# A capacity mixture that sends its results to the tokens' rows, and an attention whose loads and norms are reordered

## The chip, the cores and the metric

One core of a Trainium2 chip runs the whole program in one launch. The metric is the device time in microseconds: the median of three runs. Five engines matter below: TensorE (PE), VectorE (DVE), ScalarE (ACT), GpSimd (POOL) and SyncE (SP), which issues most DMAs.

## The reference

Four layers over x (4 x 256 tokens of 256 numbers), each of an attention and a feed-forward part on a layer norm, both added to x. The context has 4 x 1601 tokens. The parts that matter here:

```python
# layer 2, feed-forward: T = 1024 tokens, E = 8 experts, C = T / E = 128 seats each, H = 352
probs = softmax(xt @ Wg); eidx = argmax(probs); gate = probs[eidx]
oh = one_hot(eidx); pos = (cumsum(oh, 0) * oh).sum(-1) - 1      # first come, first served
keep = pos < C
flat = where(keep, eidx * C + pos, E * C)
xd = zeros(E * C, d).at[flat].set(xt, mode='drop').reshape(E, C, d)
oe = ((silu(xd @ W1) * (xd @ W3)) @ W2).reshape(E * C, d)       # an expert at a time
out = take(oe, minimum(flat, E * C - 1)) * (gate * keep)[:, None]
return out + (silu(xt @ sw1) * (xt @ sw3)) @ sw2                # a shared expert beside it

# layer 3, attention: 16 query heads, 4 key heads, head size 128
q = rms_norm(x @ Wq); k = rms_norm(ctx @ Wk); v = ctx @ Wv      # 4 query heads share a key head
y = softmax(q @ k.T / sqrt(128)) @ v @ Wo
```

Layer 1's attention is of the same kind, with the tokens of x behind the context's as keys, and with queries and keys turned by their position (rope). Layer 0 has an attention that keeps 54 scores a row and a top-2 mixture, layer 1 a linear map, layer 2 an attention of 16 heads of 16 to an image part and a text part of the context, and layer 3 a top-2 mixture with a shared expert.

## The kernel before

x stays on the chip as eight tiles `X[j]` of 128 tokens. The stages follow one another: the first attention with its mixture to about 520 us of the profile, `gqa` for layer 1 ("l1a", 520 to 1870), the linear map, the image and text attention (to 2467), `capacity_moe` (2467 to 2569), `gqa` for layer 3 ("l3a", 2570 to 3690) and the last mixture. In the stages touched here the order on PE, ACT and DVE is that of the program (`manual_schedule`; in `gqa` POOL's as well). SP's queue, and POOL's in `capacity_moe`, are ordered by a scheduler. An engine and a queue take their work strictly in order.

**The layer norm.** `normed(nat)` gives the transposed tiles `xT` and, for each of four pairs of token tiles, three steps: statistics with the reciprocal root (DVE, one pow on POOL by `rsqrt`, L122, DVE scales into `nat`, L145), PE's transposes, and the copies out of PSUM. `layernorm()` runs all of them at once.

**`capacity_moe`.** It loads the router's `wg`, the shared expert's weights `wsh` and eight experts' weights (1088 KB each), norms the four pairs into `nat[0..7]`, routes, and counts each token's seat with two PE products. `ix` gets two rows for each token tile: the seat's row, or a row past the seats for a token that found none, and the same clamped to 1023. Eight indirect stores, issued by POOL (L1897), send the tiles' rows to XD in DRAM, and eight plain loads bring an expert's 128 rows back (`xs`, L1905). Meanwhile PE runs the shared expert's first products (`up`, L1866) and first half of its second (`down(0)`). Then, one expert ahead of the other, `hidden(e)` (transposes, L1916, products L1924, silu) and `project(e)` (L1937); ACT copies the result (`oe`, L1939) and SP stores it to OE in DRAM (L1940). `down(1)` adds the shared expert's second half to `X[4..7]`. Then eight indirect loads from POOL's queue (L1951) fetch each token's row from OE, and DVE adds it, times `gate`, to `X[j]` (L1954). `gate` has been set to zero for tokens without a seat.

**Between the stages.** The last mixture's shared weights `shw` (1536 KB) are loaded first, then `layernorm()` runs, some constants are made on POOL, and `gqa` starts. `send_to_shared` gives `gqa` the hook `others`, through which the last mixture's routing is hung into its slots.

**`gqa`.** Its 16 units are a batch times a key head. A unit has four steps: a tile of 128 tokens by a pair of query heads. A step takes four slots, and a slot runs its phases in the order first, early, mid, late, last, values, pe, post: "mid" holds the row maxima (DVE, L1252) and the exponentials (ACT, L1253) of this slot's scores (PE, L1244, into three score banks `sc0..2`); `combine` (L1290 to L1298) joins the parts of the softmax and turns the blocks; `values` (L1324) multiplies by the values; the last product with `wo` is L1337. `at(slot, phase, f)` hangs anything into a slot. Slot -16 is the first, and scores start at slot -4. `produce_queries` projects (L1187), norms (`rsq`, L122; `nq`, L1208) and transposes (L1219) the queries, `produce_keys` (L1113) the keys and values. For l3a some key chunks were made in the first attention (`early`, 13, 12, 0 and 0 for the four batches) and are loaded by `load_keys`; for batch 0 these are all. `evac` copies out of PSUM, by ACT and DVE in turn. The weights of a unit:

```python
def weights(u):                                  # L1051
    for t, n in ((wkv, "_wkv"), (wq, "_wq")):
        nc.sync.dma_start(t, A[key + n]...)      # L1058: 256 KB and 512 KB for l3a's and l1a's
    nc.sync.dma_start(wo, A[key + "_wo"]...)     # 512 KB
...
weights(0); weights(1)                           # ahead of all slots; later units in a slot
```

Of the kernel before, what the change touches and what calls it, by code (L numbers as in the profile page):

```python
# [12 lines left out]
F32 = mybir.dt.float32  # L13
I32 = mybir.dt.int32
# [4 lines left out]
P = 128  # L19
B = 4  # L20
# [32 lines left out]
def kernel(ctx: ExitStack, tc: tile.TileContext, A, out: bass.AP):  # L53
# [70 lines left out]
    def normed(nat=None, bank=None):  # L124


        halves = []

        def pair(i):
            v = {}  # L130

            def scale():
                if i % 2 == 0:
                    halves.append(pools["x"].tile([P, NC_, 512], F32, tag="xlnT", name="xlnT", bufs=2))
                mv = small([P, 2, 2], "bnmv2")
                for tt in range(2):
                    st = small([P, 6], "bnst")
                    nc.vector.bn_stats(st, X[2 * i + tt])
                    nc.vector.bn_aggr(mv[:, tt], st)
                rstd = small([P, 2], "rstd2")  # L140
                rsqrt(rstd, mv[:, :, 1], 1.0, 1e-5, P, 2)
                v["xl"] = []
                for tt in range(2):
                    xl = nat[2 * i + tt] if nat is not None else small([P, D], "xl", 2)
                    nc.vector.tensor_scalar(  # L145
                        xl, X[2 * i + tt], mv[:, tt, 0:1], rstd[:, tt : tt + 1], ALU.subtract, ALU.mult
                    )
# [860 lines left out]
    def gqa(xT, key, tabs=None, early=None, others=None):  # L1008
# [14 lines left out]
        with (  # L1023
# [24 lines left out]
            def at(slot, phase, *fs):  # L1048
                todo.setdefault((slot, phase), []).extend(fs)

            def weights(u):  # L1051
                kv = u % KVH
                w = pool.tile([P, 1536], F32, tag="w", name="w")
                wo = pool.tile([P, GRP, D], F32, tag="wo", name="wo", bufs=3)
                wq = w[:, 0:1024].rearrange("p (c o) -> p c o", c=NC_)
                wkv = w[:, 1024:1536].rearrange("p (c o) -> p c o", c=NC_)
                for t, n in ((wkv, "_wkv"), (wq, "_wq")):
                    nc.sync.dma_start(t, A[key + n].rearrange("p (c h o) -> p c h o", c=NC_, h=KVH)[:, :, kv, :])  # L1058
                nc.sync.dma_start(wo, A[key + "_wo"].rearrange("p (k h o) -> p k h o", k=KVH, h=GRP)[:, kv])
                state[u] = dict(wq=wq, wkv=wkv, wo=wo)  # L1060

            def loaded(u):

# [285 lines left out]
            if others:  # L1349

                others(at, lambda b: 4 * (16 * b + 15) + 13)
            weights(0)
            weights(1)
            for u in range(units):
                made = -(-loaded(u) // 2)
                n = len(pairs) - made + 2
                t0 = 16 * (u - 1) - 4 if u else -13
                if made:
                    load_keys(u, t0)
                if u > 1:  # L1360
                    at(t0 - 3, "early", lambda u=u: weights(u))
                for g in range(n):
                    t = t0 + (g // 2 if u == 0 else g * 12 // n)
                    if g < 2:
                        produce_queries(u, g, t)
                    else:
                        produce_keys(u, made + g - 2, t)
# [430 lines left out]
        nc.vector.tensor_tensor(dst, psu, gv, ALU.mult)  # L1798


    def capacity_moe(XD, OE):

# [4 lines left out]
        with (  # L1807
# [3 lines left out]
        ):  # L1811
            wg = one.tile([P, NC_, E], F32, tag="wg", name="wg")
            nc.sync.dma_start(wg, A["l2f_wg"])

            def weights(tag, src):
                w = one.tile([P, 2176], F32, tag=tag, name=tag)
# [14 lines left out]
            nc.gpsimd.iota(base, [[CAP, E]], base=-1, channel_multiplier=0, allow_small_or_imprecise_dtypes=True)  # L1831
            lost = one.tile([P, NJ], F32, tag="lost", name="lost")
            nc.gpsimd.iota(lost, [[P, NJ]], base=LOST, channel_multiplier=1, allow_small_or_imprecise_dtypes=True)
            nat = [one.tile([P, D], F32, tag=f"nat{j}", name=f"nat{j}") for j in range(NJ)]
            xT, norm = normed(nat)
            norm[0][0]()
            for i in range(NJ // 2):
                if i + 1 < NJ // 2:
# [49 lines left out]
            ix = one.tile([P, 2, NJ], I32, tag="ix", name="ix")  # L1888
# [3 lines left out]
            nc.vector.tensor_tensor(ix[:, 0, :], f, lost, ALU.add)  # L1892
# [41 lines left out]
            def project(e, hT):  # L1934
                ps = ps_tr()
                for hc, (o, n) in enumerate(H2C):
                    nc.tensor.matmul(ps[:, :D], hT[:n, hc, :], W[e][2][:n, hc, :], start=(hc == 0), stop=(hc == 2))  # L1937
                oe = pool.tile([P, D], F32, tag="oe", name="oe")
                nc.scalar.copy(oe, ps[:, :D])  # L1939
                nc.sync.dma_start(OE[e * CAP : (e + 1) * CAP, :], oe)  # L1940

            hT = None
            for e in range(E + 1):
# [3 lines left out]
                hT = nx  # L1947
            down(1)
            for j in range(NJ):
                y = one.tile([P, D], F32, tag=f"xs{j}", name=f"y{j}")  # L1950
                nc.gpsimd.indirect_dma_start(  # L1951
                    y, None, OE[:, :], bass.IndirectOffsetOnAxis(ap=ix[:, 1, j : j + 1], axis=0)
                )
                nc.vector.scalar_tensor_tensor(X[j], y, gate[:, j : j + 1], X[j], ALU.mult, ALU.add)  # L1954

# [338 lines left out]
    OE = dp.tile([E * CAP, D], F32, tag="oe", name="oe")  # L2294
# [11 lines left out]
    with rings(0, sc=3, tr=1, acc=1):  # L2306
        image_text(layernorm())
    with rings(0, tr=3, acc=5):
        capacity_moe(XD, OE)
    with tc.tile_pool(name="sort3", bufs=1) as sortp:  # L2310
        shw = sortp.tile([P, 3072], F32, tag="shw", name="shw")
        nc.sync.dma_start(shw, A["l3f_sw"])
# [91 lines left out]
```

## Time and profile before

| | |
|---|---|
| median of 3 runs | 3754.8 us (3753.04 to 3756.34) |
| profiled execution | 3761.75 us, its span 3760.0 us |
| mean granted PE clock | 0.97 |
| PE / PE weight loads busy | 3557.2 us (95%) / 2128.8 us (57%) |
| DVE / ACT / POOL busy | 2615.3 (70%) / 1678.3 (45%) / 1311.5 us (35%) |
| DMA | 248.5 MB, mean 66 GB/s |
| the chain that ended last, by engine | PE 70%, DVE 14%, POOL 7%, issue 5%, ACT 2%, DMA 2% |

The profile is of one execution. Busy shares are means over stages with different limits. The chain is followed back from the last instruction: at each step to what released it, or to the instruction before it on its engine; "issue" is time in which nothing shown was waited for. The clock is the share of full speed that PE was granted.

### The profile page before, as it was taken

To read this page: it belongs to the slowest core of one execution; us is meant where nothing else is said; L and a number is where in the kernel's file an instruction comes from. 1 tells how busy PE (TensorE), PEld (TensorE's weight loads), DVE (VectorE), ACT (ScalarE), POOL (GpSimd) and SP (SyncE) were. 2 spreads that over 40 slices of the span, in tenths; PEclk is the share of its full clock that TensorE was granted. 3 is DMA by queue.
4 is the path that set the end of the run, shared out by engine and by line. 5 is a ranking of instruction groups with operands and counts; after the bars stand their busy time and mean duration, and the time that the engine had idled before them with its cause. 6 is when DMAs were issued, how large, how long until landed. Compare 5 with 4: busy or idle time off the path is not lost.

```text
span 3760.0 us, 63083 instructions
## 1 busy us (share of the span) xinstructions
PE 3557.2 (95%) x23397; PEld 2128.8 (57%) x23397; DVE 2615.3 (70%) x5204; ACT 1678.3 (45%) x4926; POOL 1311.5 (35%) x2091
## 2 busy tenths in 40 slices
PE   8887968999999999999999999987999999999998
PEld 4556954555555555555545555553555556556655
DVE  7894856777777777777667676525778766666664
ACT  4442645445444444444224444522444445545532
POOL 3332444444544544444321101012333433333332
PEclk9997989999999999999989999988999999999999
DMA  7326342222221222220100000033111111111103
GB/s 245 102 69 235 85 142 69 63 67 63 73 70 56 59 68 64 65 73 17 40 36 19 1 19 1 1 136 133 42 57 43 57 35 43 56 35 38 28 27 111
DMA packets 173715, 248.50 MB, mean 66 GB/s; under 512 B 21581, under 2 KB 134881, under 8 KB 169825
## 3 DMA queue, kind: packets, MB, share of 16 engines
q1 hardware_dynamic: 167025, 233.00, 19.9%
q0 software_dynamic: 6384, 11.47, 1.4%
q8 instruction: 186, 3.05, 0.3%
q14 instruction: 120, 0.98, 0.1%
HBM read 199.39 MB, written 45.03 MB: 65 GB/s over the span
## 4 chain that ended last, share of the span: by engine, by line
PE 70%; DVE 14%; POOL 7%; issue 5%; ACT 2%; DMA 2%; SPq 0%; another core or an unknown queue 0%; POOLq 0%; DVEq 0%; ACTq 0%
PE acc L1324 17%; PE sc L1244 15%; PE tr L1113 5%; PE sc L1657 4%; PE acc L1676 3%; PE tr L1187 3%; PE sc L1605 3%; DVE PT L1298 3%; POOL pe L1293 3%; PE acc L884 3%; POOL t L1160 2%; PE tr L1553 2%; PE tr L1337 2%; DVE m L521 2%; DVE work L523 1%
## 5 line engine op out<-in xcount | busy, mean ns | idle before, releaser
L1253 ACT ACTIVATE pe<-sc,ms 128x480 f32<-128x480 f32 (+1 forms) x1024 | 643.5, 631 | 892.7 <-DVE ms L1252 862.6
L1324 PE MATMUL acc<-PT,V 128*128 128x256 f32 (+1 forms) x3584 | 895.9, 390 | 6.9 <-ACT OT L1331 6.9
L1244 PE MATMUL sc<-KT,QT 128*32 128x480 f32 (+5 forms) x8192 | 883.1, 535 | 15.4 <-ACT pe L1253 12.1
L1293 POOL TENSOR_SCALAR pe<-pe,fac 128x480 f32<-128x480 f32 (+1 forms) x1024 | 654.8, 659 | 586.2 <-ACT pe L1253 213.7
L1324 PEld LDWEIGHTS acc<-PT,V 128*128 128x128 f32 (+1 forms) x3584 | 641.8, 190 | 349.4 <-issue 206.5
L1252 DVE TENSOR_REDUCE ms<-sc 128x1 f32<-128x480 f32 (+1 forms) x1024 | 607.9, 615 | 139.9 <-PE sc L1244 119.9
L1298 DVE STREAM_TRANSPOSE PT<-pe 128x1920 f32<-128x1920 f32 (+1 forms) x256 | 519.5, 2030 | 0.0
L1244 PEld LDWEIGHTS sc<-KT,QT 128*32 128x32 f32 x8192 | 220.9, 109 | 402.1 <-issue 321.8
L122 POOL TENSOR_TENSOR rs<-rsq_t,mhalf 128x2 f32<-128x2 f32 (+2 forms) x248 | 160.2, 646 | 568.6 <-DVE rsq_t L121 563.9
L1663 ACT ACTIVATE pt<-sc 128x1024 f32<-128x1024 f32 (+1 forms) x224 | 215.5, 962 | 280.7 <-PE sc L1657 245.9
L1113 PE MATMUL tr<-w,cx 128*128 128x256 f32 (+1 forms) x1264 | 303.5, 382 | 1.3 <-ACT nk L1129 1.3
L1619 DVE TENSOR_REDUCE mx<-sc 128x2 f32<-128x982 f32 (+2 forms) x224 | 211.6, 957 | 98.9 <-PE sc L1605 65.8
L1113 PEld LDWEIGHTS tr<-w,cx 128*128 128x128 f32 (+1 forms) x1264 | 226.7, 187 | 31.6 <-ACT nk L1129 2.0
L1657 PE MATMUL sc<-QT,KT 32*128 32x256 f32 (+1 forms) x1664 | 240.4, 403 | 0.0
L1605 PE MATMUL sc<-KT,QT 32*128 32x491 f32 (+4 forms) x1024 | 236.9, 564 | 0.0
L1253 ACT ACTIVATION_READ_ACCUMULATOR pe<-sc,ms 128x1 f32 x1024 | 199.4, 195 | 0.0
L1657 PEld LDWEIGHTS sc<-QT,KT 32*128 32x128 f32 (+1 forms) x1664 | 139.2, 182 | 92.8 <-issue 72.9
L1121 ACT ACTIVATE sq<-tr 128x128 f32<-128x128 f32 (+1 forms) x348 | 96.8, 278 | 171.5 <-PE tr L1113 166.4
L122 POOL TENSOR_TENSOR rsq<-rsq_t,mhalf 128x4 f32<-128x4 f32 x64 | 65.2, 1018 | 308.5 <-DVE rsq_t L121 308.5
L1676 PE MATMUL acc<-pt,vbuf 128*32 128x256 f32 (+1 forms) x1792 | 142.5, 391 | 0.0
L1161 DVE TENSOR_TENSOR nk<-nk,tab 128x256 f32<-128x256 f32 (+1 forms) x128 | 65.6, 513 | 100.2 <-POOL t L1160 99.0
L1187 PE MATMUL tr<-w,xlnT 128*128 128x512 f32 x256 | 126.1, 618 | 3.8 <-DMA wo<-in_l1a_wo 3.1
(430 smaller groups left out, 4774.5 us busy)
## 6 DMA issues: line engine op xcount, KB each, us to landing
cx<-in_ctxT SPq DMA_DIRECT2D x144, 256.0 KB, 3.0
tab<-rope SPq DMA_DIRECT2D x112, 256.0 KB, 2.7
w<-in_l0f_w SPq DMA_DIRECT2D x8, 2048.0 KB, 19.8
ctxT<-in_ctxT SPq DMA_DIRECT2D x7, 1601.0 KB, 6.5
w<-in_l2f_w SPq DMA_DIRECT2D x8, 1088.0 KB, 8.2
w<-in_l1a_wq SPq DMA_DIRECT2D x16, 512.0 KB
wo<-in_l1a_wo SPq DMA_DIRECT2D x16, 512.0 KB, 4.8
w<-in_l3a_wq SPq DMA_DIRECT2D x16, 512.0 KB, 7.3
```

The lines of the kernel that those rows point to most:

```text
L122: nc.gpsimd.tensor_tensor(dst, t[:n, :k], mhalf[:n, :k], ALU.pow)
L1113: nc.tensor.matmul(v["ps"][:n, i, :], lhs, st["wkv"][:, c, :], start=(c == 0), stop=(c == NC_ - 1))
L1187: nc.tensor.matmul(v["ps"], xtok(xT, b * 2 + tt, c), state[u]["wq"][:, c, :], start=(c == 0), stop=(c == NC_ - 1))
L1244: nc.tensor.matmul(sc[32 * r : 32 * r + 32, 0 : lens[r]], st["QT"][:, tt, o : o + 32], st["KT"][:, r, 0 : lens[r]], start=True, stop=True,)
L1252: nc.vector.tensor_reduce(top, sc, AX.X, ALU.max, negate=True)
L1253: nc.scalar.activation(w, sc, AF.Exp, bias=top, accum_out=s)
L1293: nc.gpsimd.tensor_scalar(w, w, v["fac"][:, g * 4 + a : g * 4 + a + 1], 1.0, ALU.mult, ALU.mult)
L1298: nc.vector.transpose(state[steps[i]][:, :, g * P : (g + 1) * P].rearrange("p k (a t) -> p a k t", a=4), pes[g].rearrange("p a (k i) -> p ...
L1324: nc.tensor.matmul(v["ps"][:, 0 : 2 * P], V[:n, k, :], PT[:n, k, :], start=(k == 0), stop=(k == nch - 1))
L1605: nc.tensor.matmul(st[:, j, c : c + n], QT[r, g, tt * P : (tt + 1) * P], KT[r, g, o : o + n], start=True, stop=True,)
L1657: nc.tensor.matmul(st[:n, j, q, :], KT[r, g, o : o + n], QT[r, :], start=True, stop=True)
L1676: nc.tensor.matmul(acc[32 * j : 32 * j + 32, a, :], V[:n, place, h * VW : h * VW + 32], pt[:n, j, q, :], start=(k == 0), stop=(k == nch - ...
```

## The change

In `capacity_moe` a seat's row in DRAM is longer by four numbers and carries the token's index and its gate beside its norm. The rows go to XS, whose rows were of that length already. An empty seat reads, from a store that precedes, an index past the tokens and a gate of zero. The expert's result is scaled by the gate as ACT copies it, and an indirect store from POOL, one an expert, sends its rows to the tokens' rows of XD, which a store of zeros has cleared. At the end eight plain loads, on SP's and ACT's queues in turn, fetch the token tiles' rows, and DVE adds them to `X[j]`. OE is gone, and so is the second row of `ix`.

In `gqa`, for both attentions that use it, a unit's loads go out as `wq`, `wkv`, `wo`; `wkv` only where the unit makes keys of its own. Units 0 and 1: `wq` and `wkv` of unit 0 at once, its `wo` and all of unit 1 at slot -12.

Between the two, only the first pair of tiles is normed ahead of l3a. The other three stand in its slots: statistics in "late" of slots -3, 1 and 5, the transposes in "pe" of the slot behind, the copies in "early" of the one after that. `shw` is loaded at slot 12.

```diff
@@ gqa, weights
-                for t, n in ((wkv, "_wkv"), (wq, "_wq")):
-                    nc.sync.dma_start(t, ...)
-                nc.sync.dma_start(wo, ...)
+                for t, n in ((wq, "_wq"), (wkv, "_wkv")):
+                    if n == "_wq" or 2 * -(-loaded(u) // 2) < nch:
+                        nc.sync.dma_start(t, ...)
+                return lambda: nc.sync.dma_start(wo, ...)
@@ gqa
-            weights(0)
-            weights(1)
+            at(-12, "early", weights(0), lambda: weights(1)())
...
-                    at(t0 - 3, "early", lambda u=u: weights(u))
+                    at(t0 - 3, "early", lambda u=u: weights(u)())
@@ capacity_moe
+            none = one.tile([P, E, 2], F32, tag="none", name="none")
+            nc.gpsimd.memset(none, 0.0)
+            nc.gpsimd.iota(none[:, :, 0], [[CAP, E]], base=B * S, channel_multiplier=1, ...)
+            nc.sync.dma_start(XS[0:LOST, D : D + 2].rearrange("(e p) d -> p e d", p=P), none)
+            zero = one.tile([P, D], F32, tag="zero", name="zero")
+            nc.gpsimd.memset(zero, 0.0)
+            nc.sync.dma_start(XD[0 : B * S, :]..., zero.unsqueeze(1).to_broadcast([P, NJ, D]))
...
-            nat = [one.tile([P, D], F32, tag=f"nat{j}", name=f"nat{j}") for j in range(NJ)]
-            xT, norm = normed(nat)
+            nat = [one.tile([P, ROW], F32, tag=f"nat{j}", name=f"nat{j}") for j in range(NJ)]
+            for j in range(NJ):
+                nc.gpsimd.iota(nat[j][:, D : D + 1], [[0, 1]], base=j * P, channel_multiplier=1, ...)
+                nc.gpsimd.memset(nat[j][:, D + 2 :], 0.0)
+            xT, norm = normed([t[:, 0:D] for t in nat])
...
+            for j in range(NJ):
+                nc.gpsimd.tensor_copy(nat[j][:, D + 1 : D + 2], gate[:, j : j + 1])
...
-            nc.vector.scalar_tensor_tensor(f, row, 1.0 - LOST, line, ALU.add, ALU.mult)
-            nc.vector.tensor_scalar(ix[:, 1, :], f, LOST - 1.0, 1.0, ALU.add, ALU.mult)
-            nc.vector.tensor_tensor(gate, gate, line, ALU.mult)
             for j in range(NJ):
                 ins = nc.gpsimd.indirect_dma_start(
-                    XD[:, :], bass.IndirectOffsetOnAxis(ap=ix[:, 0, j : j + 1], axis=0), nat[j], None
+                    XS[:, :], bass.IndirectOffsetOnAxis(ap=ix[:, j : j + 1], axis=0), nat[j], None
...
-                x = one.tile([P, D], F32, tag=f"xs{e}", name=f"xs{e}")
-                nc.sync.dma_start(x, XD[e * CAP : (e + 1) * CAP, :])
+                x = one.tile([P, ROW], F32, tag=f"xs{e}", name=f"xs{e}")
+                nc.sync.dma_start(x, XS[e * CAP : (e + 1) * CAP, :])
...
-                oe = pool.tile([P, D], F32, tag="oe", name="oe")
-                nc.scalar.copy(oe, ps[:, :D])
-                nc.sync.dma_start(OE[e * CAP : (e + 1) * CAP, :], oe)
+                oe = pool.tile([P, D], F32, tag="oe", name="oe", bufs=4)
+                nc.scalar.activation(oe, ps[:, :D], AF.Copy, scale=xs[e][:, D + 1 : D + 2])
+                to = small([P, 1], "y_to", 4).bitcast(I32)
+                nc.vector.tensor_copy(to, xs[e][:, D : D + 1])
+                nc.gpsimd.indirect_dma_start(XD[:, :], bass.IndirectOffsetOnAxis(ap=to, axis=0), oe, None)
...
             for j in range(NJ):
-                y = one.tile([P, D], F32, tag=f"xs{j}", name=f"y{j}")
-                nc.gpsimd.indirect_dma_start(y, None, OE[:, :], bass.IndirectOffsetOnAxis(ap=ix[:, 1, j : j + 1], axis=0))
-                nc.vector.scalar_tensor_tensor(X[j], y, gate[:, j : j + 1], X[j], ALU.mult, ALU.add)
+                y = one.tile([P, ROW], F32, tag=f"xs{j}", name=f"y{j}")[:, 0:D]
+                (nc.sync, nc.scalar)[j % 2].dma_start(y, XD[j * P : (j + 1) * P, :])
+                nc.vector.tensor_tensor(X[j], y, X[j], ALU.add)
@@ between the stages
-        nc.sync.dma_start(shw, A["l3f_sw"])
...
-            xT = layernorm()
+            xT, pairs = normed()
+            for f in pairs[0]:
+                f()
             k = sort_constants(sortp)
-            r, batch, others = send_to_shared(sortp, k, XS)
+            r, batch, routes = send_to_shared(sortp, k, XS)
+            def others(at, done):
+                routes(at, done)
+                at(12, "early", lambda: nc.sync.dma_start(shw, A["l3f_sw"]))
+                for p, t in zip(pairs[1:], (-3, 1, 5)):
+                    for f, slot, phase in zip(p, (t, t + 1, t + 2), ("late", "pe", "early")):
+                        at(slot, phase, f)
```

More of the change, by code (lines that the diff above doesn't have):

```diff
@@ L1056, in weights @@
                 wkv = w[:, 1024:1536].rearrange("p (c o) -> p c o", c=NC_)
-                for t, n in ((wkv, "_wkv"), (wq, "_wq")):
-                    nc.sync.dma_start(t, A[key + n].rearrange("p (c h o) -> p c h o", c=NC_, h=KVH)[:, :, kv, :])
-                nc.sync.dma_start(wo, A[key + "_wo"].rearrange("p (k h o) -> p k h o", k=KVH, h=GRP)[:, kv])
+                for t, n in ((wq, "_wq"), (wkv, "_wkv")):
+                    if n == "_wq" or 2 * -(-loaded(u) // 2) < nch:
+                        nc.sync.dma_start(t, A[key + n].rearrange("p (c h o) -> p c h o", c=NC_, h=KVH)[:, :, kv, :])
                 state[u] = dict(wq=wq, wkv=wkv, wo=wo)
+                return lambda: nc.sync.dma_start(
+                    wo, A[key + "_wo"].rearrange("p (k h o) -> p k h o", k=KVH, h=GRP)[:, kv]
+                )
             def loaded(u):
@@ L1798, in gated, with capacity_moe @@
         nc.vector.tensor_tensor(dst, psu, gv, ALU.mult)
-    def capacity_moe(XD, OE):
+    def capacity_moe(XS, XD):
         ET = mybir.EngineType
@@ L1813, in capacity_moe @@
             nc.sync.dma_start(wg, A["l2f_wg"])
+            none = one.tile([P, E, 2], F32, tag="none", name="none")
+            nc.gpsimd.memset(none, 0.0)
+            nc.gpsimd.iota(
+                none[:, :, 0], [[CAP, E]], base=B * S, channel_multiplier=1, allow_small_or_imprecise_dtypes=True
+            )
+            nc.sync.dma_start(XS[0:LOST, D : D + 2].rearrange("(e p) d -> p e d", p=P), none)
+            zero = one.tile([P, D], F32, tag="zero", name="zero")
+            nc.gpsimd.memset(zero, 0.0)
+            nc.sync.dma_start(
+                XD[0 : B * S, :].rearrange("(j p) d -> p j d", p=P), zero.unsqueeze(1).to_broadcast([P, NJ, D])
+            )
             def weights(tag, src):
@@ L1833, in capacity_moe @@
             nc.gpsimd.iota(lost, [[P, NJ]], base=LOST, channel_multiplier=1, allow_small_or_imprecise_dtypes=True)
-            nat = [one.tile([P, D], F32, tag=f"nat{j}", name=f"nat{j}") for j in range(NJ)]
-            xT, norm = normed(nat)
+            nat = [one.tile([P, ROW], F32, tag=f"nat{j}", name=f"nat{j}") for j in range(NJ)]
+            for j in range(NJ):
+                nc.gpsimd.iota(
+                    nat[j][:, D : D + 1], [[0, 1]], base=j * P, channel_multiplier=1,
+                    allow_small_or_imprecise_dtypes=True,
+                )
+                nc.gpsimd.memset(nat[j][:, D + 2 :], 0.0)
+            xT, norm = normed([t[:, 0:D] for t in nat])
             norm[0][0]()
@@ L1887, in capacity_moe @@
             nc.vector.tensor_scalar(line, line, CAP + 0.5, 1.0, ALU.is_lt, ALU.mult)
-            ix = one.tile([P, 2, NJ], I32, tag="ix", name="ix")
+            ix = one.tile([P, NJ], I32, tag="ix", name="ix")
             f = small([P, NJ], "c_f", 1)
@@ L1891, in capacity_moe @@
             nc.vector.tensor_tensor(f, f, line, ALU.mult)
-            nc.vector.tensor_tensor(ix[:, 0, :], f, lost, ALU.add)
-            nc.vector.scalar_tensor_tensor(f, row, 1.0 - LOST, line, ALU.add, ALU.mult)
-            nc.vector.tensor_scalar(ix[:, 1, :], f, LOST - 1.0, 1.0, ALU.add, ALU.mult)
-            nc.vector.tensor_tensor(gate, gate, line, ALU.mult)
+            nc.vector.tensor_tensor(ix, f, lost, ALU.add)
             for j in range(NJ):
                 ins = nc.gpsimd.indirect_dma_start(
-                    XD[:, :], bass.IndirectOffsetOnAxis(ap=ix[:, 0, j : j + 1], axis=0), nat[j], None
+                    XS[:, :], bass.IndirectOffsetOnAxis(ap=ix[:, j : j + 1], axis=0), nat[j], None
                 ).ins
@@ L1937, in project @@
                     nc.tensor.matmul(ps[:, :D], hT[:n, hc, :], W[e][2][:n, hc, :], start=(hc == 0), stop=(hc == 2))
-                oe = pool.tile([P, D], F32, tag="oe", name="oe")
-                nc.scalar.copy(oe, ps[:, :D])
-                nc.sync.dma_start(OE[e * CAP : (e + 1) * CAP, :], oe)
+                oe = pool.tile([P, D], F32, tag="oe", name="oe", bufs=4)
+                nc.scalar.activation(oe, ps[:, :D], AF.Copy, scale=xs[e][:, D + 1 : D + 2])
+                to = small([P, 1], "y_to", 4).bitcast(I32)
+                nc.vector.tensor_copy(to, xs[e][:, D : D + 1])
+                ins = nc.gpsimd.indirect_dma_start(
+                    XD[:, :], bass.IndirectOffsetOnAxis(ap=to, axis=0), oe, None
+                ).ins
+                tc.declare_no_dep(ins, group="results", reason="no two seats have the same token's row")
+                tc.add_to_no_dep_group("results", ins)
             hT = None
@@ L1949, in capacity_moe @@
             for j in range(NJ):
-                y = one.tile([P, D], F32, tag=f"xs{j}", name=f"y{j}")
[L1951 to L1954, printed above, removed]
+                y = one.tile([P, ROW], F32, tag=f"xs{j}", name=f"y{j}")[:, 0:D]
+                (nc.sync, nc.scalar)[j % 2].dma_start(y, XD[j * P : (j + 1) * P, :])
+                nc.vector.tensor_tensor(X[j], y, X[j], ALU.add)
     WIDE3 = 4 * I3 + D
@@ L2293 @@
     XD = dp.tile([2 * ROOM, D], F32, tag="xd", name="xd")
-    OE = dp.tile([E * CAP, D], F32, tag="oe", name="oe")
     OQ = dp.tile([(E + MORE) * P, D], F32, tag="oq", name="oq")
@@ L2308 @@
     with rings(0, tr=3, acc=5):
-        capacity_moe(XD, OE)
+        capacity_moe(XS, XD)
     with tc.tile_pool(name="sort3", bufs=1) as sortp:
         shw = sortp.tile([P, 3072], F32, tag="shw", name="shw")
-        nc.sync.dma_start(shw, A["l3f_sw"])
         with rings(0, sc0=1, sc1=1, sc2=1, tr=4, acc=1):
-            xT = layernorm()
+            xT, pairs = normed()
+            for f in pairs[0]:
+                f()
             k = sort_constants(sortp)
-            r, batch, others = send_to_shared(sortp, k, XS)
+            r, batch, routes = send_to_shared(sortp, k, XS)
[5 more added lines that the diff above has]
+                        at(slot, phase, f)
             gqa(xT, "l3a", early=(EARLY, KD, VD), others=others)
```

## The prediction

> **What bounds the kernel now.** I read the page first, then the chain of waits around the places the diff touches, then the queue and engine timelines there. PE is busy 95% of the span, so an edit pays only where PE stands. The seam between the capacity mixture and the next attention is such a place; its chain:
>
> ```profile
> 2554.08 2.61 PE tr L1866 x12
> ...
> 2561.03 0.95 POOL y L1951
> ...
> 2566.03 3.14 DMA y<-oe,ix
> 2569.17 0.03 issue
> 2569.19 0.49 DVE x L1954
> ...
> 2571.29 8.39 DMA w<-in_l3a_wq
> 2579.69 0.14 issue
> 2579.82 6.12 PE tr L1187 x8
> ```
>
> (start, length, what). PE's last shared product ends at 2559.28. Then eight gathers go out one by one from POOL, the last token tile is added at 2569.67, and only then do the loads of the next attention start; PE's first query projection waits for its weights until 2579.82. The SP queue shows why that load takes 8.39 us:
>
> ```profile
> 2569.81 0.33 SPq L2312 DMA_DIRECT2D shw<-in_l3f_sw  x1
> 2570.19 0.43 SPq L1963 DMA_DIRECT2D wg<-in_l3f_wg  x1
> 2570.67 0.58 SPq L1058 DMA_DIRECT2D w<-in_l3a_wkv  x1
> 2571.29 0.71 SPq L1058 DMA_DIRECT2D w<-in_l3a_wq  x1
> ```
>
> 1536 KB of `shw`, not used for 1000 us, and 256 KB of `wkv` lie ahead of it. The first attention starts alike: its `wkv` is issued at 521.70, its `wq` at 522.35, and PE's first L1187 is at 528.55, though its last norm transpose ended at 525.41.
>
> **The change, part by part.** The profiled execution took 3761.75 us (span 3760.0), 7 us over the median of the runs, 3754.8. I work out a difference against the former and take it off the latter.
>
> *Gathers out, scatters in.* The expert loop gets per expert one ACTIVATE with a scale in place of a COPY (0.37), a one-column DVE copy and an indirect store on POOL. PE carries that loop (L1924 2.92, L1937 1.30 of each 4.96 us); DVE waits 0.8 us an expert for PE, POOL has no work from 2507 to 2557. Cost nothing; uncovered, 8 x 0.3. No table load comes with it: in the first attention a Copy with a scale (`nk`, L1129) stands among exponentials without one. The last result leaves ACT at 2554.53, so its store starts at 2554.7. From start to the release of readers I take 2.4 us: the last seat store (L1897) started at 2506.01 and the loads behind it at 2508.39. The eight plain loads, four on SP and four on ACT, go out 0.43 us apart from 2557.1 and land after 1.9 (`xs<-xd`) to 2.5 us (`x<-xd`): the first at 2559.0 to 2559.6, the last at 2560.3 to 2560.9. DVE adds the shared product until 2559.74, then does eight adds of 0.42 to 0.48 (L181, L1954): the last ends at 2563.2, where it was 2569.67. Gain 6.4.
>
> *Loads in order of use.* Now only `wg` stands ahead of `wq`. 256 KB land in 3.0 to 3.1 us, 512 KB of `wo` in 4.8; I take 4.3 for `wq` alone. Issued at 2563.8 it is there at 2568.1. What comes last then is the norm: 4.83 us lay between the last add and the first pair's `xlnT` (2574.50). That chain stays (13 POOL constants, pow, scale, transposes, copy) and gets one DVE step ahead of the pow, 0.2. So `xlnT` at 2568.2, PE at 2568.4 to 2568.8: I take 11.2 of gain up to there, both parts together. `shw` goes to slot 12, where DMA is 8% busy (2626 to 2660); `wkv` is dropped for batch 0, whose keys are ready.
>
> *Norms in slots.* Pairs 1 to 3 ran under the wait for `wq`; now each stands in DVE's order at slots -3, 1 and 5 of the attention. One pair is the stretch from 2471.39 to 2474.30:
>
> ```profile
> 2471.39 0.42 DVE L138 BATCH_NORM_STATS2 bnst<-x 128x6 f32<-128x256 f32 x1
> ...
> 2472.59 0.17 DVE L121 TENSOR_SCALAR rsq_t<-bnmv 128x2 f32<-128x2 f32 x1
> 2473.56 0.74 DVE L145 TENSOR_SCALAR nat<-x,bnmv,rstd 128x256 f32<-128x256 f32 x2 [0.81 <-POOL rstd L122]
> ```
>
> 2.9 us in which DVE does nothing else, 0.8 of it waiting for POOL's pow. Queued behind are the row maxima (L1252), behind them ACT's exponentials, which free the three score banks, and so PE. What slack is there?
>
> ```profile
> 2595.88 1.08 DVE L1252 TENSOR_REDUCE ms<-sc 128x1 f32<-128x416 f32 x2
> 2597.15 1.13 DVE L1208 SCALAR_TENSOR_TENSOR nq<-tr,rsq,qw 128x128 f32<-128x128 f32 x4 [0.20 <-POOL rsq L122]
> 2598.20 1.08 DVE L1252 TENSOR_REDUCE ms<-sc 128x1 f32<-128x416 f32 x2
> ...
> 2605.10 1.07 DVE L1252 TENSOR_REDUCE ms<-sc 128x1 f32<-128x416 f32 x2
> 2606.10 0.14 DVE L1290 COPY fac<-tr 128x8 f32<-128x8 f32 x1
> ```
>
> At slot -3 the hold stands between the first two rows: 0.2 of slack, 2.7 lost. At slot 1, between the last two: about 0.4 of slack, 2.5 lost. At slot 5 the values have begun and DVE waits for PE (2.91 us at 2626.98): about 1.0 lost. Two of three transposes of four (0.6 each for `nq`, L1219) run in the holds; the third costs 0.3. Because `evac` alternates, the first QT is now copied by DVE behind its eight `nq` (2589.73) rather than by ACT: 0.4. Sum 6.9, between 0 if DVE's idle third took it (13.28 us busy of 20 from 2592) and 9.1, three whole holds and the 0.4. Nearest are the rows shown, so 6.9.
>
> *First attention.* `wq` is issued at 521.70 and lands at 526.0 by the same 4.3; the norm transposes allow 525.5. Gain 2.5, between 0 and 3.0. What follows hangs on engines, not loads, so it lasts: the tightest load is the sixth context block, now behind a table load that waits for DVE's first rotation (549.72, less 2.5); it lands near 550.5 for a use at 556.22 less 2.5, 3 us to spare. The later units' new order costs nothing: in the whole first attention PE waits for weights once, 3.1 us, at this start.
>
> *Front of the mixture.* 19 small POOL steps (0.05 to 0.2 each, as the constants at 2570) come ahead of the second pair's pow at 2470.00; POOL was free from 2468.05: 0.3 lost, up to 0.8. A 1 MB store of zeros and 1024 short rows precede the weights; at 422 GB/s that is 2.5 us, against a first use of `wsh` at 2485.1 with all nine blocks moved by 2494: nothing. Rows of 1040 instead of 1024 bytes land in 2.1 us (sparse mixture) instead of 1.9; PE has 3 us to spare at 2513.4: nothing. Three DVE steps of 0.2 fall away off the path.
>
> Sum: -11.2 + 6.9 - 2.5 + 0.3 = -6.5 us, 3755.2 for the profiled execution, 3748.3 for the median.
>
> **Rivals.** *The norms hide.* DVE is idle a third of slots -3 to 2; if the holds fall there, only the 0.4 remains: -11.2 + 0.4 - 2.5 + 0.3 = -13.0, 3741.8. For it: between 2606 and 2610 DVE stands four times. Against: it stands for PE and ACT, which wait for it in turn.
>
> *The clock falls in each hold.* PE's clock falls to half when it idles:
>
> ```profile
> 2612.00:2619.00 7.00, 3.36 (x30) 1.03 (x30) 6.71 (x13) 2.44 (x9) 0.34 (x1) 0.99 0.19 67
> 2619.00:2626.00 7.00, 6.07 (x27) 2.49 (x31) 3.63 (x9) 2.68 (x8) 4.31 (x8) 0.52 0.00 0
> ```
>
> (stretch, us, PE, PEld, DVE, ACT, POOL busy, clock, DMA). PE is half idle in the first and at clock 0.52 in the next: 16 score products take 3.23 us, not 1.59, six value products 2.75, not 1.56. That is 2.8 a fall. Two further falls, in the holds at slots -3 and 1, make +5.6: -0.9, 3753.9. The Trainium skill (TensorE: Matmul & The Clock Gate, Part 1) says the same of the cause: an idle window of about 3.4 us halves the clock and a busy one restores it. By that rule a hold of 2.9 us with part of a window idle around it may or may not bring a fall; the rows above agree with it.
>
> *The clock stays at half.* From 1926 to 1957 it stood at 0.51 for 31 us with PE busy 28.5 of them. If the hold at slot -3 brings such a stretch, the 20.6 us of PE work in the 27 us from 2592 to 2619 take 41.2: +14.2, with the sum above +7.7, 3762.5: slower. It decides beyond 13 us of PE work at half clock, as the first 6.4 us fill idle time and the next 6.5 eat the gain. The page just named gives one busy window for the way back, so by it this would not last; the row from 1926 is against the page.
>
> **How the numbers follow.** Main case 0.50, with seam 10.2 to 11.7, holds 5 to 8.5, first attention 1 to 3: 3745 to 3752, a bit over a third of it below 3747.3. Norms hidden 0.27; a fall in each hold 0.14; half clock 0.09. A measurement of this kernel can tell about 0.2%, 7.5 us, from no change. Faster by more: 0.18 + 0.27 = 0.45. Within: 0.32 + 0.14 = 0.46. Slower: 0.09. The range takes in the hidden norms and the falls: 3740.5 to 3756.
>
> **What would show it.** Right: the last add of the mixture near 2563 and PE's first L1187 some 11 us earlier than 2579.82; then the first value product (L1324) only 4 to 5 us earlier than 2623.26; in the first attention L1187 at about 526. Wrong: the first L1324 earlier by 9 or more (the norms hide); more stretches of half clock from 2580 to 2615; a `wq` that lands after `xlnT`; or a wait of PE for `xs`, `wsh` or a context load.

## The result and the profile after

The changed kernel takes 3746.8 us (median of 20 runs, 3742.6 to 3752.3), the kernel before in the same comparison 3755.5 (20 runs). The ratio is 0.9978, interval 0.9972 to 0.9985: 8.3 us less, between 5.6 and 10.5. Forecast were 3748.3, 6.5 less. The profiled execution took 3746.33, span 3744.6, clock 0.975.

The chain at the seam, as before (start, length, what):

```profile
2545.48 2.40 DMA xd<-oe,y_to
...
2548.93 4.40 DMA y<-xd
...
2554.44 0.43 DVE x L1977
...
2555.43 5.26 DMA w<-in_l3a_wq
2560.70 0.80 issue
2561.50 5.37 PE tr L1190 x8
```

The last scatter lands 2.40 us after its start, as priced. The first plain load lands after 2.5 us, but the one that DVE waits for last takes 4.40. `wq`, with only `wg` ahead, takes 5.26 and 0.80 more until PE starts, not 4.3. The plain loads by queue (KB each, median us from issue to landing):

```profile
y<-xd ACTq DMA_DIRECT2D x4, 128.0 KB, 2.5
y<-xd SPq DMA_DIRECT2D x4, 128.0 KB, 3.6
```

The SP queue there:

```profile
2555.05 0.33 SPq L1986 DMA_DIRECT2D wg<-in_l3f_wg  x1
2555.43 0.58 SPq L1059 DMA_DIRECT2D w<-in_l3a_wq  x1
2556.06 0.59 SPq L1084 DMA_DIRECT2D KT<-keys  x1
2556.70 0.43 SPq L1085 DMA_DIRECT2D V<-values  x1
...
2568.13 0.41 SPq L2343 DMA_DIRECT2D shw<-in_l3f_sw  x1
```

The key tile (832 KB) and the values (768 KB) follow `wq` within 1.3 us. And `shw`, hung into slot 12 (about 2640), left at 2568.13: a slot binds the engines whose order is written out, and SP's is not. What was hung into slot -12, unit 0's `wo` and unit 1's loads, likewise left at 2557.67 to 2558.77, while `wq` was on its way. The first norm in a slot, on DVE (start, length, line, operation):

```profile
2577.98 1.08 DVE L1255 TENSOR_REDUCE ms<-sc 128x1 f32<-128x416 f32 x2
2578.98 0.42 DVE L138 BATCH_NORM_STATS2 bnst<-x 128x6 f32<-128x256 f32 x1
...
2581.16 0.73 DVE L145 TENSOR_SCALAR xl<-x,bnmv,rstd 128x256 f32<-128x256 f32 x2 [0.81 <-POOL rstd L122]
2581.81 1.12 DVE L1211 SCALAR_TENSOR_TENSOR nq<-tr,rsq,qw 128x128 f32<-128x128 f32 x4
2582.84 1.08 DVE L1255 TENSOR_REDUCE ms<-sc 128x1 f32<-128x416 f32 x2
```

From the end of one pair of row maxima to the start of the next are 3.8 us; before, they were 1.2.

**Where the time went.** The two programs run the same PE products, so the k-th product of a line can be set against the k-th of the same line: the difference of starts is PE's lead. From the first profile of before to that of the changed kernel it grows by 2.4 at the start of the first attention (by 600), falls by 1.1 through that attention, grows by 1.4 in the linear map, 7.2 at the start of the image attention, 2.7 over the mixture's front and the seam, and 1.5 at the last mixture. 1.8 more lie behind PE's last product, and 0.3 are lost in the first 500 us: 15.4 us of span in all. That is nearly twice what the medians differ by, so one profile of each tells too much.

### The profile page after: what moved, and what is told of

Its sections match the earlier page's. It is cut to its first block, busy times and chain, and to the rows that moved or that the text cites. A ratio compares the mean times of both kernels' runs of the same rounds, so it can differ in the third digit from the quotient of the medians.

```text
span 3744.6 us, 63118 instructions
## 1 busy us (share of the span) xinstructions
PE 3547.3 (95%) x23397; PEld 2123.0 (57%) x23397; DVE 2613.3 (70%) x5209; ACT 1681.2 (45%) x4926; POOL 1317.5 (35%) x2118
## 4 chain that ended last, share of the span: by engine, by line
PE 69%; DVE 14%; POOL 8%; issue 5%; DMA 2%; ACT 2%; SPq 1%; POOLq 0%; DVEq 0%; ACTq 0%
PE acc L1327 17%; PE sc L1247 15%; PE tr L1116 5%; PE sc L1659 4%; PE acc L1678 3%; PE tr L1190 3%; POOL pe L1296 3%; DVE PT L1301 3%; PE sc L1607 3%; PE acc L884 3%; POOL t L1163 2%; PE tr L1340 2%; PE tr L1555 2%; DVE m L521 2%; DVE work L523 1%
## 5 line engine op out<-in xcount | busy, mean ns | idle before, releaser
L1190 PE MATMUL tr<-w,xlnT 128*128 128x512 f32 x256 | 125.8, 616 | 4.8 <-DMA w<-in_l3a_wq 2.7
## 6 DMA issues: line engine op xcount, KB each, us to landing
w<-in_l0f_w SPq DMA_DIRECT2D x8, 2048.0 KB, 15.4
```

The source lines that it names most:

```text
L1190: nc.tensor.matmul(v["ps"], xtok(xT, b * 2 + tt, c), state[u]["wq"][:, c, :], start=(c == 0), stop=(c == NC_ - 1))
```

## Experiments

All leads in the table are of PE against the first profile of before: "L1190" from the mixture's last products to the first query projection of the second attention, "seam" to the products from 3000 on, where the lead is constant. Two numbers are two profiles. Ratios are against the kernel before on the same chip. The split version at 9, 13, 17 was run five times in each comparison, that with `wq` early eight times, the changed kernel first 20 times, the others eleven times.

| kernel | L1190 | seam | ratio (95%) |
|---|---|---|---|
| before, second profile | -0.2 | 0.7 | (one run) |
| changed | 8.9; 9.1 | 2.8; 5.2 | 0.9978 (0.9972 to 0.9985); 0.9981 (0.9972 to 0.9990) |
| load order alone | 0.6 | 1.7 | 0.9991 (0.9982 to 1.0000) |
| mixture alone | 5.0 | 6.2 | 0.9984 (0.9975 to 0.9993) |
| shw first | 5.8 | 1.6 | 0.9992 (0.9983 to 1.0001) |
| norms ahead | 6.5; 6.7 | 7.1; 7.4 | 0.9981 (0.9972 to 0.9990); 0.9980 (0.9971 to 0.9989) |
| norms at 9, 13, 17 | 9.0 | 7.1 | 0.9976 (0.9967 to 0.9985) |
| split at -3, 1, 5 | 9.1 | 7.7 | 0.9981 (0.9972 to 0.9990) |
| split at 9, 13, 17 | 9.1; 9.1 | 9.0; 8.3 | 0.9965 (0.9951 to 0.9979); 0.9966 (0.9952 to 0.9979) |
| the same, wq early | 11.2 | 11.4 | 0.9968 (0.9958 to 0.9979) |

**The kernel before, a second profile.** No edit.

> The kernel before once more, for a second profile of it. Theory (clock luck): the 31 us of half clock at the start of the image attention (1926 to 1957), the slow 1.5 us near 3681 and the 1.1 us by which PE's lead shrank through the first attention are of that one execution; a second one shows them shorter or not at all, and its span is nearer 3754 than 3760. Rival (the edits removed them by moving the phase): the second profile repeats them within 1 us.

The span was 3757.6. The stretch at the image attention, first in the first profile of before, then in the second, then in the changed kernel (stretch, length, busy PE, PEld, DVE, ACT, POOL, clock, DMA share, GB/s):

```profile
1932.00:1940.00 8.00, 7.01 (x20) 2.37 (x16) 6.40 (x11) 0.51 (x2) 0.54 (x1) 0.50 0.00 0
1948.00:1956.00 8.00, 8.00 (x40) 4.20 (x34) 3.73 (x4) 3.07 (x3) 0.00 (x0) 0.50 0.01 2
```
```profile
1932.00:1940.00 8.00, 7.70 (x40) 3.83 (x40) 6.78 (x12) 0.51 (x2) 0.00 (x0) 0.76 0.00 0
1948.00:1956.00 8.00, 8.00 (x40) 4.44 (x40) 4.20 (x4) 3.07 (x3) 0.00 (x0) 0.50 0.01 2
```
```profile
1932.00:1940.00 8.00, 4.83 (x22) 2.48 (x22) 6.62 (x11) 0.00 (x0) 0.55 (x1) 0.79 0.00 0
1948.00:1956.00 8.00, 8.00 (x94) 4.69 (x88) 6.40 (x11) 4.47 (x6) 1.33 (x3) 1.00 0.00 0
```

The unbroken 31 us at half clock became two falls, 3.1 us shorter in all: that part was of the one execution. Against the second profile of before, the twelve profiles of the edited kernels still gained between 1.3 and 4.2 us at this start, all with the same code there. Both profiles of before are slower than its median, by 7 and 5 us, so leads outside the seam overstate what a version gains; why all twelve gain here is not shown. The 1.1 us lost through the first attention are of single executions too: the version with the mixture's edits alone, whose first attention is untouched, loses 1.0, and the second profile of the changed kernel 0.1. The 1.5 us at 3681 did come back: there the rival held. First before, then changed:

```profile
3680.83 7.34 PE L2155 MATMUL tr<-shw,acts 128*128 128x256 f32 x26 [2.80 <-DVE acts L1798]
3668.71 5.88 PE L2178 MATMUL tr<-shw,acts 128*128 128x256 f32 x26 [2.80 <-DVE acts L1800]
```

After the same wait for DVE the 26 products take 7.34 and 7.47 us in the two profiles of before, 5.88 in both of the changed kernel; in the second profiles the granted clock behind the wait was 0.57 (3680 to 3684) and 1.00 (3668.5 to 3672.5). Of the twelve profiles of edited kernels seven gain these 1.5 us and five do not: mixture alone, norms ahead (both), norms at 9, 13, 17 and split at -3, 1, 5. The Trainium skill (TensorE: Matmul & The Clock Gate, Part 1) says that the activity window runs freely, so that the same kernel meets it at different points; the differing stretches at 1932 agree, the repeated 1.5 us are not explained by it.

**The changed kernel again, and its parts alone.**

> The changed kernel once more, beside the two versions with other places for the norms. Theory: 0.9978 of before again (8 us), and at the seam the same steps as in its first profile: first L1190 8.9 us earlier against the mixture's PE work, 3.2 and 1.9 us lost in the first two holds, 2.8 us gained at the first value products. Rival (the holds' price was luck of that profile): the net gain at the seam differs by more than 2 us.

The first step repeats (9.1). The first two holds cost 2.5 and 1.9 (3.2 and 1.9 in the first profile), and 0.7 more are lost behind the second in both. At the first value product the lead is 5.2 instead of 2.8: 2.4 us apart, over the bound that was set for the rival. Of this, 1.1 stand between the first L1190 and the first hold, where the granted clock was 0.76 from 2570 to 2577 in the first profile and 1.00 from 2572 to 2579 in the second. Another 0.7 stand at the end of the first hold: there the clock fell in the first profile (0.61 from 2583 to 2586) and stayed at 1.00 in the second. So a single profile of this seam is good to about 2 us. In this second profile the mixture's front lost 1.7 us, most of it at half clock, which the first did not.

The 0.7 behind the second hold are not the third one, which begins on DVE at 2608.74. They are in the chain of the first profile:

```profile
2598.71 0.61 POOL pe L1296
2599.32 1.00 POOL rsq L122
2600.34 0.10 DVE nq L1211
```

A small copy (`fac`) stood behind the norm on DVE, so POOL's eight scalings that need it began 1.02 us after the norm's pow. The pow of the next queries (`rsq`) stood behind the scalings, and DVE waited 1.19 us for it (1.18 in the second profile, 0.23 in before). This is read from the chain; no run moves `fac` alone. The third hold itself cost PE nothing but its four transposes, 0.4.

> Only the edits inside gqa on the kernel before (wq first, wkv only where keys are made, wo and unit 1 at slot -12); the mixture, the norms and shw as before. Theory (the terms of the prediction): the first attention starts its L1187 2.4 us earlier and keeps it; in the second attention wq still stands behind shw and the transposes of the last norm pair end at 2579.16 of before, so at most 0.6 us more. Sum -3.0 us, a median near 3752.5. Rival (given back): in the changed kernel PE's lead shrank by 1.1 us between 550 and 1860; if that is the price of the new order in the later units, the sum is -1.9 us, and the lead shrinks here too. Rival (clock luck): the half-clock stretch from 1926 to 1957 of before, absent from the changed kernel's profile, comes and goes by the execution; then it may be there or not in this run, whose edits do not touch that place.

0.9991 is 3.4 us less, 3.0 forecast. The seam shows L1190 0.6 us earlier, as said; the first attention 3.0 us at its start (516 to 568), in the changed kernel 1.7 and 2.7. The lead shrinks by 1.1 through the rest of that attention here too; but it shrinks as much where that code is untouched, and by no more than 0.2 in six other profiles with this order, so it is not the order's price.

> Only the edits of the capacity mixture on the kernel before (rows with index and gate, scatters, plain loads); loads of the attentions, shw ahead and the four norm pairs as before. Theory: the last add of the mixture ends 5.4 us earlier against the mixture's own PE work, and everything behind it (shw, wq, norms, L1187) keeps its distance, since wq still waits behind shw; the front costs 0.3. Sum -5.1 us, a median near 3750.4. Rival (the loads in order are needed for any of it): wq's landing is held by something else than the last add, then less than 2 us.

0.9984 is 6.0 less, 5.1 forecast. L1190 comes 5.0 earlier, and without holds the lead does not fall behind it (6.2 at the seam's end).

**The load of shw first again.**

```diff
+        nc.sync.dma_start(shw, A["l3f_sw"])   # ahead of the norms
-                at(12, "early", lambda: nc.sync.dma_start(shw, A["l3f_sw"]))
```

> The changed kernel with the load of shw (1536 KB) ahead of all others at the seam again, as before the change; wq still ahead of wkv, norms in slots. Theory: the first L1190 waits for wq, and wq for shw's bytes: at the 409 GB/s that the queue moved from 2578 to 2585 before, 1536 KB are 3.8 us, of which the start of the transfers hides about 1; so L1190 comes 2.5 to 3.8 us later than the 6.6 us after the last add that the changed kernel took, at 9.1 to 10.4, and the seam gains 2.5 to 3.8 us less. Rival (wq's landing does not hang on what stands ahead of it): 6.6 us after the last add, no change.

The first L1190 comes 10.35 us after the last add (2555.05 to 2565.40), 3.7 later than in the changed kernel:

```profile
2555.23 0.33 SPq L2334 DMA_DIRECT2D shw<-in_l3f_sw  x1
2555.61 0.43 SPq L1986 DMA_DIRECT2D wg<-in_l3f_wg  x1
2556.09 0.58 SPq L1059 DMA_DIRECT2D w<-in_l3a_wq  x1
```

The issue of `wq` moved by 0.5 us against the last add; what moved the landing are the bytes ahead. So of the 3.9 us that the load order and the norms in slots bring together at L1190 beside the mixture's edits (8.9 less 5.0), 3.1 go when `shw` is put ahead again (8.9 less 5.8). At the seam's end this version nets 1.6, which is 1.2 and 3.6 less than the two profiles of the changed kernel.

**Where the norms stand.** Ahead of the attention (`xT = layernorm()` again), and at later slots (`(9, 13, 17)` for `(-3, 1, 5)`):

> The changed kernel with all four norm pairs ahead of the second attention again; shw stays at slot 12, everything else as changed. Theory (the holds cost what the trace shows): PE's first L1187 of the second attention comes behind the fourth pair's transposes, 9.5 us after the last add as in before, so near 2564.4 in place of 2561.5, 2.9 later; the three holds of DVE, which cost 6.1 to 6.5 us by PE's lead between its first L1187 and its first value product, are gone. Net 3.2 us faster than the changed kernel, near 3743.6. Rival (the holds hide, the lead was lost otherwise): 2.9 us slower than the changed kernel, near 3749.7.

> The changed kernel with the three norm pairs at slots 9, 13 and 17 instead of -3, 1 and 5, nothing else. Theory: at -3 and 1 PE has no other work than scores that wait for DVE's row maxima, and loses 3.2 and 1.9 us; from slot 6 on value products stand between the scores, PE is busy all the time and the three score banks cover part of a hold: at most 0.5 us each, as the hold at slot 5 showed. Net 5 us faster than the changed kernel, near 3741.8. Rival (a hold of 2.9 us costs the same wherever it stands): no change against the changed kernel, near 3746.8.

> The version with all four pairs ahead of the attention once more. Its lead at the seam was 7.1 us where the changed kernel had 2.8 and 5.2 in two profiles, yet its median came out no lower. Theory (the seam counts, the median was at the edge of its interval): beside the same before it is 0.9968 to 0.9975, 2 to 4 us better than the changed kernel's 0.9978 to 0.9981. Rival (something else takes it back): 0.998 again, and a place in this profile where PE's lead falls by 2 to 4 us that the other versions keep.

With all pairs ahead L1190 is 2.5 us later (2.9 forecast), and nothing is lost behind it: the seam nets 7.1 and 7.4. So the holds of the change cost more than they brought, 2 to 4.6 us by the seam. The medians do not show it: 0.9981 and 0.9980, no lower than the changed kernel, where 3 us and then 2 to 4 us less had been forecast. One part of the reason was found: at 3681 this version takes 7.4 us for the 26 products, as before, and gives 1.5 us back. Whether the remaining 0.4 to 3 us are there cannot be told within an interval of 3.4 us either way.

At 9, 13 and 17 the losses are 0.7, 0.4 and 0.4, and 1.0 more at 2661 of this kernel: 2.6, where at most 1.5 were forecast. The net, 7.1, is that of all pairs ahead, and the median (0.9976) is the changed kernel's within the interval, not 5 us below it. The last 1.0 comes by way of POOL, after the third hold, as in the changed kernel after the second:

```profile
2652.03 4.74 POOL L1296 TENSOR_SCALAR pe<-pe,fac 128x416 f32<-128x416 f32 x8 [1.02 <-DVE fac L1293]
2656.72 1.02 POOL L122 TENSOR_TENSOR rsq<-rsq_t,mhalf 128x4 f32<-128x4 f32 x1
```

Again `fac` stood behind the norm on DVE, POOL's scalings began 1.02 us after the pow, `rsq` stood behind them, and DVE waited 1.16 us for it.

**Split norms.**

```diff
-    scale()                       # statistics, pow, scaling: one piece
+    stats(); apply()              # "late" of slot t and of slot t + 1
-    evac(xlnT, ps)                # ACT and DVE in turn
+    nc.scalar.copy(xlnT, ps)      # and the turn set as if the copies had been made ahead
```

> The changed kernel with the norm pairs at slots 9, 13 and 17, each in two parts: statistics in one slot, scaling in the next, so that DVE does not stand waiting for POOL's pow; ACT alone copies these three out, and the turn of the copies elsewhere is that of before. Theory: at slots 9 to 17 the whole pairs lost 1.6 us in three steps of about 0.5, most of it PE's own four transposes (0.44), and 1.0 more where the turn of the copies had changed; split, 1.3 us stay (three times PE's transposes). Seam net 8.2 us in place of 7.1, so about 1 us faster than the version with whole pairs at 9, 13 and 17, and 5 us faster than the changed kernel by the lead at the seam. Rival (DVE's work itself is the price, not its wait): no better than with whole pairs, 7.1 us.

> The version with split norms at slots 9, 13 and 17 once more, beside the others on the same chip. Theory: 0.9965 to 0.9970 of before, the lead at the seam 8.5 to 9.5 us, and 2 us better than all pairs ahead. Rival (its first median was luck): 0.998, no better than the changed kernel.

DVE in the split version; two maxima now stand between statistics and scaling, and nothing waits for POOL:

```profile
2614.66 0.41 DVE L139 BATCH_NORM_STATS2 bnst<-x 128x6 f32<-128x256 f32 x1
...
2616.00 1.08 DVE L1267 TENSOR_REDUCE ms<-sc 128x1 f32<-128x416 f32 x2
2617.00 1.18 DVE L149 TENSOR_SCALAR xl<-x,bnmv,rstd 128x256 f32<-128x256 f32 x2
```

PE's lead falls by 0.44 three times, once per pair: its own four transposes and nothing else. (The 1.0 was put to the turn of the copies in the expectation. That was wrong: DVE copies QT there in both versions and in before; with the scaling a slot later, `fac` no longer stands behind it, and POOL's scalings follow the pow at once.) The ratio, 0.9965 and 0.9966, is the lowest of all kernels run: 13 us less than before, and 4 to 7 less than versions run beside it (3740.1 to the changed kernel's 3747.3; 3743.3 to 3747.1 with all pairs ahead), 1.5 of the latter at 3681.

> The changed kernel with its norm pairs where they are, at slots -3, 1 and 5, but each in two parts as in the split version (statistics in one slot, scaling in the next, transposes in the one after, ACT copying out). It tells the wait inside a hold from the place of the hold. Theory (DVE standing 2.9 us is the price, and 0.8 of it is the wait for POOL): the parts are 1.4 and 0.7 us, DVE's slack there was 0.2 to 0.4, so about 1.3 and 0.4 a pair at -3 and 1, and little at 5: 3.4 us lost where the whole pairs lost 4.5 to 5.1, seam net 6 us. Rival (the place decides): as much lost as with whole pairs, seam net 3 to 5 us. Rival (only the wait counts): nothing lost, seam net 9 us as at slots 9 to 17.

Split at the old slots, 3.1 us are lost from the first hold to the first value product (3.4 forecast), where whole pairs lost 4.6 and 5.7. Behind it 0.7 come back on balance, so the seam nets 7.7 and not 6: the value products ran at 0.21 us each where they took 0.43 in before and in the changed kernel, as the clock had fallen and risen again earlier (0.71 from 2609 to 2612, in the first profile of the changed kernel 0.55 from 2610 to 2613). By these leads both rivals are out. But the edit did two things: it took out the wait for POOL, and it gave the copies of `xlnT`, 0.68 us of DVE a pair in the changed kernel, to ACT. What each is worth was not told apart. The way by POOL stayed: the norm's pow stands ahead of its scalings, and DVE waited 1.78 us for `rsq`. The median (0.9981) is no lower than the changed kernel's; 1.5 us of that are at 3681. That the place counts shows in the medians too: run beside the version split at 9, 13 and 17, all eleven times here (3745.9 to 3749.7) lie above all five there (3740.8 to 3745.8).

> The same as the version with split norms at slots 9, 13 and 17, and the first unit's wq loaded into a tile of its own during the mixture, with the experts' weights. Theory: PE's first L1190 of the second attention waited for wq until 2561.50 while the norm's transposed pair was there at 2559.45; the wait goes, L1190 starts 2 us earlier, and the lead stays: 2 us faster than without it. Rival (another load takes its place: the keys or the second unit's): the first scores, which need the key tile issued after wq, then wait, and the gain at the first score product is under 0.7 us. Rival (the mixture pays): the 512 KB among the experts' weights delay the shared products' weights; then PE's lead in the mixture falls by over 1 us.

L1190 starts 2.1 us earlier and the seam keeps it, 11.4. The first rival is out: the first score product gains as much. The front of the mixture lost 1.6 us in this profile, but so it did in the second profile of the changed kernel and of the split version, with no `wq` there, so the last rival is neither shown nor excluded. In the medians the 2 us do not show (0.9968 beside 0.9965): they are within the intervals.

## Why the prediction was right, step by step

- **Last add: mis-sized.** 6.4 forecast, 5.4 measured. The step that failed is the landing of the plain loads, put at 1.9 to 2.5 us for each of the eight. They are 1 MB together: they left from 2547.9 on and the last was there at 2553.3, 5.4 us later; from 2549 to 2553 the DMA engines were busy 0.81 of the time and moved 246 GB/s. The 1.9 was the landing of the first of the eight loads `xs`, which go out on one queue 0.47 us apart; in the second profile of before the last of them landed after 2.88, 6.1 us after the first had left. So the second queue saved 0.7 us. The Trainium skill (DMA: Bandwidth & Descriptors, Issuing engines are not separate DMA queues) says that transfers issued by several engines interleave on the same sixteen DMA engines, so two queues save issue time only; the 5.4 us beside 6.1 agree.
- **`wq` in 4.3 us: mis-sized.** It took 6.1 with the wait behind it (5.8 and 5.0 in the first attention). The 1536 KB of `shw` ahead of it made 3.7 more; what the loads behind it cost was not tested. The order of two landings was turned with it: `xlnT` was there at 2559.45, as the chain of the norm said (4.6 us after the last add, 5.0 forecast), and `wq` at 2561.50. The prediction named this as a sign of being wrong, and here it was. With `wq` loaded ahead, 2.1 us came back. The gain up to L1190 was 8.9, not 11.2.
- **Norms in slots: right in kind, too high.** 2.7, 2.5 and 1.0 for the holds and 0.7 for a transpose and a copy were forecast, 6.9. Measured were 2.5 to 3.2 and 1.9 in the first two and 0.4, PE's transposes, at the third; 0.7 by way of POOL, which the forecast did not have; and a little given back: 4.6 and 5.7 in all. The slack of 0.2 and 0.4 at the first two was about rightly read. The copy of QT, 0.4 forecast, shows as 0.3 ahead of the holds (beside the versions whose copies have their old turn).
- The two errors, 2.1 to 2.3 too much gain and 1.2 to 2.3 too much loss, cancel: -4.3 forecast for both, -2.8 and -5.2 measured. That the sum fits is partly luck.
- **First attention: the sum right, the landing mis-sized here too.** 2.5 were forecast at its first product. PE's first L1190 came 1.1 and 1.9 earlier there (1.4 to 2.0 in the other kernels with that order), at 527.8 and 526.8 and not at 526; up to 568 it was 1.7 and 2.7 (2.2 to 3.3). The rest of the gain came behind the start with the clock (from 550 to 555 it was 0.62 in before and 0.90 in the changed kernel), which the forecast did not have.
- **Front: 0.3 forecast.** 0.1 in one profile of the changed kernel, 1.7 in the other. 1.3 to 1.7 appear in six of eleven profiles with the mixture's edits and in none of three without. A clock that rises later makes it: 0.62 from 2479 to 2484 in the second profile of the changed kernel, 0.92 from 2488 to 2493, over about the same products, in the second of before. Whether the edits make that likelier was not settled.
- **Hold for loads at slot 12: wrong, at no cost seen.** `shw` left 70 us before that slot.
- **The rivals.** "The norms hide" asked for a first value product 9 us or more earlier: with the 9.4 us of the stages before the seam taken off, it came 2.8 earlier (2611.05 for 2623.26). "The clock stays at half" did not come: from 2584 to 2605 the granted clock was 0.90 to 1.00. "The clock falls in each hold" came once: behind the first hold in one profile of two (0.61 from 2583 to 2586), at a price of 0.7 and not 2.8; behind the second hold it stayed at 1.00 in both.

The 2 us between 6.5 and 8.3 are within the interval. The repeated 1.5 us at 3681 would fill most of it; why the clock falls there for some kernels and not for others stays open.

## What to carry to other kernels

Price loads that leave together by their bytes and by the landing of the last, not of the first. Work that is moved off a wait into a loop is better cut where it waits for another engine, and put where the bound engine has other products to do: the same three norms cost 4.6 to 5.7 us, then 3.1 (cut, with the copies on ACT, up to the first value product), 2.6 (moved) and 1.3 (both), the last being PE's own part. And compare two profiles of the same kernel before explaining a difference in a stage that no edit touches.

## What the runs showed that was not expected

Half clock at a single place (31 us at 0.50 from 1926 on, about 20 us in two pieces in a second execution) made 3.1 us between two profiles of the same kernel, and 7.2 between the first profiles of the two kernels, near to the whole effect of this change. And a hold of DVE was paid twice: once by the maxima behind it, and once, 0.7 to 1.0 us, by way of POOL, whose 4.7 us of work ahead of the next pow waited for a small copy behind the hold.
